# A two-layer transformer on one core: one tile for the output's sums of all passes, weights' sums at other slots, additions a slot apart, and a branch's number read sooner

## The chip, the cores and the metric

The kernel runs on one core of one Trainium2 chip. The time is the device time of one execution in microseconds (us), lower is better. The kernel before took 2757.16, 2756.16 and 2751.43 us in three runs; the median is 2756.16. Everything is in 32-bit floats.

The engines are written as in the profile: PE is TensorE (matmuls), ACT is ScalarE, DVE is VectorE, POOL is GpSimd, SP is the engine whose queue issues most of the transfers. A tile that a matmul writes (names ps_a, ps_b, ps_e, ps_sc, ps_o) lies in PSUM, and another engine must have read it before PE may fill it again.

## The reference

Two layers over 2048 tokens of 512 features. Each layer is attention plus a feed-forward part on the normalised input. The change touches only the first layer's attention (32 heads of 128):

```
qkv   = silu(xn @ qkv_w.T)                  # per head: q, k, v
per block of 32 tokens, with a state kv:
  out = (q k^T * diag_decay) v + (q * q_decay) kv
  kv  = kv * block_decay + (k * k_decay)^T v
attn  = norm_w * out_all * rsqrt(mean(out_all^2) + eps)
x1    = x + (sigmoid(xn @ gate_w.T) * attn) @ out_w.T + experts(xn)
```

The feed-forward part of layer one picks 2 of 16 experts for each token. Layer two is a 4-head softmax attention over sequences of 512, and 16 of 64 low-rank adapters for each token.

## The kernel before, in words

**Tiling.** Layer one's attention goes in four passes of 512 tokens (two sequences of 256), called pass 1 to pass 4 here; in the code the index `i` runs from 0, so pass 2 is `i == 1`. A pass has eight units `g`, 0 to 7, of four heads. A unit multiplies the tokens with that unit's weights for q, k, v and gate. This matrix product is done in sevenths, as Strassen and Winograd do: seven products of sums of blocks (`p1` to `p7`) in place of eight, and the sums that make up the results. In a unit the seven outer products come in the order p1, p2, p6, p5, p3, p7, p4 (the class `Outer`). From pass 2 on each of them is itself done sevenfold (in pass 1 only some are). That makes 49 small products in a unit, each of eight 128x128x256 matmuls in PE's records (L738), about 0.89 us, and around them the small attention of the four heads. A unit of pass 2 takes about 74.5 us.

In the span, the first decay load of pass 2 is at 707.3 us and that of pass 3 at 1303.4; pass 4 begins near 1880, and layer two near 2470.

**What happens to a product.** ACT copies one PSUM tile out (`copied`, L1112, cp<-ps_a), DVE adds the next to it, and DVE and POOL add the sum r to the results c (L101 is the line of the helper `add`). For p7 each of the four results is added twice: POOL adds r to the tile c, and DVE adds r to the tile a. The DVE additions are kept in a list `added`; three are issued together at the third result, and the fourth at the last. When a whole quarter of the results is complete, ACT makes silu and the gate (L835 to L842), PE makes scores and attends (L860/861, L872/873), DVE multiplies the scores by the decay (s, L101) and makes the gated result gT (L893), ACT squares and POOL sums the squares (sums), and POOL makes sums of gT for the next product.

**The output.** gT times the output's weights (L950, `project`) is sevenfold as well. The seven products are summed over the eight units in one tile `acc` of seven slots: unit 0 writes a slot by a copy on ACT (L958), later units add on DVE. Each pass takes its own tile from the pool `accp`, which has one buffer. After a pass, in unit 0 of the next, POOL combines the sevenths (`combine`, acc<-acc), and DVE adds them to the residual (`finish`, L649, spare<-acc,rms,spare).

**The output's weights.** Four of the seven products need sums of two weight blocks (wo<-wo). In pass 2 they are made by POOL in `out_sum` and each is stored to HBM by a transfer on SP (L1011, wos<-wo); the later passes load them. `load_out` loads the plain blocks, at the fourth, fifth and sixth outer product of the unit (k = 3, 4, 5).

**The order.** After each of the 49 products `slot()` is called. `later(after, f)` queues a piece of work for a later slot, and `slot` takes what is due: one piece, or two when over 12 wait, not counting pieces in a list of cheap names. The program order of ACT and POOL is the order in which the kernel issues (they are scheduled by hand); PE, DVE and SP are ordered by a planner by its own costs. Each engine then runs its instructions strictly in that order.

**The branch.** The router's number of expert tiles is known only at run time. In pass 4 each engine loads it (L1215) and jumps over extra experts if the usual number is enough (`beyond`, L1216).

## Time and profile before

| | us |
|---|---|
| median of three runs | 2756.16 |
| the profiled execution | 2759.92 |
| its span | 2758.2 |
| PE busy | 2704.0 (98%) |
| DVE busy | 1597.3 (58%) |
| POOL busy | 1652.5 (60%) |
| ACT busy | 943.9 (34%) |
| 32 weights' sums on POOL (wo<-wo) | 43.8 |
| mean granted TensorE clock | 0.994 |

A line of a timeline gives the start, the duration, the engine, the program's line, the operation, the tile written and the tiles read, how many instructions are drawn together, and in brackets how long the engine had been idle before it and what released it. A line of the list of waits gives the engine, what it wanted to do, after the arrow what it waited for, then microseconds in total, how often, and the longest.

### The profile page before, as it was taken

To read this page: it belongs to the slowest core of one execution; us is meant where nothing else is said; L and a number is where in the kernel's file an instruction comes from. 1 tells how busy PE (TensorE), PEld (TensorE's weight loads), DVE (VectorE), ACT (ScalarE), POOL (GpSimd) and SP (SyncE) were. 2 spreads that over 40 slices of the span, in tenths; PEclk is the share of its full clock that TensorE was granted. 3 is DMA by queue.
4 is the path that set the end of the run, shared out by engine and by line. 5 is a ranking of instruction groups with operands and counts; after the bars stand their busy time and mean duration, and the time that the engine had idled before them with its cause. 6 is when DMAs were issued, how large, how long until landed. Compare 5 with 4: busy or idle time off the path is not lost. (4 is left out here: it accounts for less than half of the span.)

```text
span 2758.2 us, 48688 instructions
## 1 busy us (share of the span) xinstructions
PE 2704.0 (98%) x19250; PEld 2499.6 (91%) x19250; DVE 1597.3 (58%) x2701; ACT 943.9 (34%) x1672; POOL 1652.5 (60%) x1509
## 2 busy tenths in 40 slices
PE   9999999999999999999999999999999999999999
PEld 5699999999999999999999999999998999987877
DVE  7656777776545555555545555555454555667663
ACT  5232222222343333333433333334433333432211
POOL 6478777776466767666755555656655567653210
PEclk9999999999999999999999999999999999999999
DMA  7898888888888777667777776787776688653211
GB/s 290 314 345 323 317 330 330 326 319 323 340 286 293 265 277 275 256 243 285 279 255 260 252 260 251 265 297 254 267 266 231 241 301 300 220 222 104 75 60 64
DMA packets 150872, 721.46 MB, mean 262 GB/s; under 512 B 18240, under 2 KB 24768, under 8 KB 108096
## 3 DMA queue, kind: packets, MB, share of 16 engines
q1 hardware_dynamic: 135824, 661.89, 65.2%
q0 software_dynamic: 14528, 55.88, 6.1%
q8 instruction: 154, 2.52, 0.4%
q14 instruction: 78, 0.64, 0.1%
q10 hardware_dynamic: 288, 0.52, 0.1%
HBM read 576.29 MB, written 144.04 MB: 261 GB/s over the span
## 5 line engine op out<-in xcount | busy, mean ns | idle before, releaser
L738 PE MATMUL ps_a<-xt,w 128*128 128x128 f32 x5376 | 752.1, 277 | 16.6 <-ACT cp L1112 11.8
L738 PEld LDWEIGHTS ps_a<-xt,w 128*128 128x128 f32 x5376 | 687.3, 193 | 44.5 <-ACT cp L1112 16.0
L101 POOL TENSOR_TENSOR c<-c,r 128x512 f32<-128x512 f32 x264 | 362.4, 1396 | 161.2 <-DVE r L101 157.7
L101 POOL TENSOR_TENSOR c<-c 128x512 f32<-128x512 f32 x240 | 305.8, 1286 | 254.4 <-DVE c L101 230.5
L1112 ACT COPY cp<-ps_a 128x512 f32<-128x512 f32 x384 | 224.2, 584 | 645.9 <-PE ps_a L738 620.0
L738 PE MATMUL ps_e<-xt,w 128*128 128x128 f32 x2688 | 376.1, 277 | 0.2 <-DVE r L101 0.2
L101 POOL TENSOR_TENSOR sums<-sums,sq 128x256 f32<-128x256 f32 x240 | 180.3, 751 | 307.7 <-ACT sq L884 297.9
L738 PE MATMUL ps_a<-w,xt 128*128 128x128 f32 x1792 | 348.0, 276 | 0.0
L738 PEld LDWEIGHTS ps_e<-xt,w 128*128 128x128 f32 x2688 | 342.9, 193 | 3.6 <-DVE r L101 0.4
L101 POOL TENSOR_TENSOR w<-w 128x512 f32<-128x512 f32 x224 | 298.2, 1339 | 76.4 <-DVE w L101 29.1
L950 PE MATMUL ps_sc<-wo,gT 128*128 128x256 f32 x1288 | 306.9, 382 | 5.2 <-PEq L1216 3.8
L738 PEld LDWEIGHTS ps_a<-w,xt 128*128 128x128 f32 x1792 | 273.3, 193 | 0.0
L101 DVE TENSOR_TENSOR acc<-ps_sc,acc 128x512 f32<-128x512 f32 x208 | 142.7, 689 | 207.0 <-PE ps_sc L950 164.2
L950 PEld LDWEIGHTS ps_sc<-wo,gT 128*128 128x128 f32 x1288 | 233.9, 192 | 31.6 <-issue 4.4
L893 DVE SCALAR_TENSOR_TENSOR gT<-ps_o,nw,c 128x256 f32<-128x256 f32 x256 | 112.0, 479 | 231.0 <-ACT sq L884 230.9
L738 PE MATMUL ps_b<-xt,w 128*128 128x128 f32 x1536 | 215.6, 277 | 6.0 <-issue 3.8
L101 DVE TENSOR_TENSOR c<-ps_a,c 128x512 f32<-128x512 f32 x216 | 146.8, 687 | 123.3 <-PE ps_a L738 117.6
L835 ACT ACTIVATE c<-c 128x512 f32<-128x512 f32 x256 | 150.2, 628 | 165.5 <-DVE c L101 108.0
L884 ACT ACTIVATE sq<-ps_o 128x512 f32<-128x512 f32 x128 | 76.5, 597 | 380.2 <-PE ps_o L873 371.8
L738 PEld LDWEIGHTS ps_b<-xt,w 128*128 128x128 f32 x1536 | 196.5, 193 | 9.2 <-issue 5.6
L101 DVE TENSOR_TENSOR s<-ps_sc,decay 128x384 f32<-128x384 f32 x256 | 139.1, 552 | 75.7 <-PE ps_sc L861 74.1
L738 PE MATMUL ps_e<-w,xt 128*128 128x128 f32 x896 | 174.1, 276 | 0.0
(296 smaller groups left out, 4581.7 us busy)
## 6 DMA issues: line engine op xcount, KB each, us to landing
w<-in_w_att_dram SPq DMA_DIRECT2D x56, 1024.0 KB
w<-in_w_att_dram SPq DMA_DIRECT2D x72, 768.0 KB
st<-in_w_att_dram SPq DMA_DIRECT2D x32, 1024.0 KB
wo<-in_w_out_dram SPq DMA_DIRECT2D x113, 256.0 KB
decay<-dec SPq DMA_DIRECT2D x64, 384.0 KB
w<-ws0p SPq DMA_DIRECT2D x12, 1792.0 KB
w<-ws1p SPq DMA_DIRECT2D x12, 1792.0 KB
w<-ws2p SPq DMA_DIRECT2D x12, 1792.0 KB
```

Source lines behind the costliest of these rows:

```text
L101: (eng or nc.vector).tensor_tensor(o, a, b, op)
L738: mm(bank[:, bass.ts(ty, P)], a, b, start=(first and ty == 0), stop=True, skip_group_check=True,)
L835: nc.scalar.activation(qk, qk, AF.Silu)
L884: nc.scalar.activation(sq, po, AF.Square)
L893: nc.vector.scalar_tensor_tensor(gT[:, h, :].rearrange("p (t n) -> p t n", t=2), po[:, bass.ts(h, S)].rearrange("p (t n) -> p t n", t=2), ...
L950: mm(py[:, bass.ts(t, S)], self.O[p][:, hh, bass.ts(t, P)], self.wo[p][:, hh, :], start=(t == 0 and hh == 0), stop=(hh == 1), skip_group_c ...
L1112: nc.scalar.copy(c, bank)
```

## The change

1. `acc` is one tile for all passes, taken once (`sums_of_seven`).
2. The output weights' sums of the second pass: the last plain block is loaded at k = 4 in place of k = 5, and the four sums are queued 6, 22, 24 and 26 slots later (slots 34, 50, 52, 54 of the unit, the last three in the next unit) in place of slots 41, 43, 45, 47.
3. p7's additions to the tile a: of the three that were issued together at the third result, one is issued at once, and the others are queued for one and two slots later; they count as cheap pieces. The fourth stays at the last result.
4. The branch's number is loaded at the start of the unit before the one that branches.

```diff
+    whole_acc = []
+
+    def sums_of_seven():
+        if not whole_acc:
+            whole_acc.append(accp.tile([P, 7, 2, C // 2], FP, tag="acc", name="acc"))
+        return whole_acc[0]
...
-                n += getattr(f, "func", f).__name__ not in ("bias_sum", "silu", "bias", "gate", "fill_tile", "read_table", "take_table", "scatter", "load_sum", "sums1", "sums2", "sums3", "sums4", "settle0", "settle1", "out_sum", "combine", "finish", "store")
+                n += getattr(f, "func", f).__name__ not in ("add_a", "bias_sum", "silu", "bias", "gate", "fill_tile", "read_table", "take_table", "scatter", "load_sum", "sums1", "sums2", "sums3", "sums4", "settle0", "settle1", "out_sum", "combine", "finish", "store")
...
                 if self.i not in acc:
-                    acc[self.i] = accp.tile([P, 7, 2, C // 2], FP, tag="acc", name="acc")
+                    acc[self.i] = sums_of_seven()
...
-                for p in {2: ("p1",), 3: ("p7", "p4", "p5"), 4: ("p6", "p2"), 5: ("p3",)}.get(k, ()):
+                for p in {2: ("p1",), 3: ("p7", "p4", "p5"), 4: ("p6", "p2", "p3")}.get(k, ()):
...
-                if k == 5 and self.i == 1:
+                if k == 4 and self.i == 1:
                     for n in range(4):
-                        later(6 + 2 * n, partial(self.out_sum, n))
+                        later((6, 22, 24, 26)[n], partial(self.out_sum, n))
...
+        def add_a(a, r):
+            add(a, a, r)
...
-                        self.added.append(partial(add, a, a, r))
-                        if (i, j) in ((1, 1), (0, 1)):
-                            while self.added:
-                                self.added.pop(0)()
+                        self.added.append(partial(add_a, a, r))
+                        if (i, j) == (1, 1):
+                            for n in range(3):
+                                later(n, self.added.pop(0)) if n else self.added.pop(0)()
+                        elif (i, j) == (0, 1):
+                            self.added.pop(0)()
...
+        n_used = []
+
         def beyond():
-            n_used = nc.values_load(used[0:1, 0:1], min_val=0, max_val=NMT)
-            with tc.If(n_used > USUAL):
+            with tc.If(n_used[0] > USUAL):
...
+            if (i, g, k) == (NCH - 1, NG - 6, 1):
+                n_used.append(nc.values_load(used[0:1, 0:1], min_val=0, max_val=NMT))
             if (i, g, k) == (NCH - 1, NG - 5, 1):
                 assert not todo
                 beyond()
```

More of the change, by code (lines that the diff above doesn't have):

```diff
@@ L974, in project_plain @@
                 if self.i not in acc:
-                    acc[self.i] = accp.tile([P, 7, 2, C // 2], FP, tag="acc", name="acc")
+                    acc[self.i] = sums_of_seven()
                 o = acc[self.i][:, 2 * b : 2 * b + 2, t]
```

## The prediction

> **What bounds the kernel now.** I read the share of busy time first, then the slices, then the list of what TensorE waited for.

> ```profile
> span 2758.2 us, 48688 instructions
> PE 2704.0 (98%) x19250; PEld 2499.6 (91%) x19250; DVE 1597.3 (58%) x2701; ACT 943.9 (34%) x1672; POOL 1652.5 (60%) x1509
> PEclk9999999999999999999999999999999999999999
> ```

> TensorE (PE) is busy 98% of the span at full clock, and the change has as many matmuls as before. So it can only give back, or add, gaps between matmuls, and the wait list of PE prices them (total us, times, longest).

> ```profile
> PE ps_a L738 <- ACT cp L1112: 11.8, 6, 2.6
> PE ps_o L872 <- DVE s L101: 6.2, 6, 2.6
> PE ps_b L738 <- issue: 3.8, 2, 2.0
> PE ps_sc L950 <- PEq L1216: 3.8, 1, 3.8
> PE ps_sc L950 <- POOL gT L101: 1.4, 1, 1.4
> ```

> The first row is the largest: six times a product waits for a PSUM tile that ScalarE (ACT) has not yet copied out. PE's timeline puts these at 125.23 (1.83 us, in the opening, which no edit touches), 1156.19 (1.77), 1230.73 (1.77), 1305.27 (1.11), 1360.30 (2.65) and 1938.35 (2.65). The last five are 9.95 us, of two kinds.

> At 1360.30, and alike at 1938.35, one unit into passes 3 and 4:

> ```profile
> 1359.18 0.58 ACT L958 COPY acc<-ps_sc 128x512 f32<-128x512 f32 x1 [8.66 <-DVE spare L649]
> 1360.30 0.94 PE L738 MATMUL ps_a<-xt,w 128*128 128x128 f32 x6 [2.65 <-ACT cp L1112]
> 1355.66 3.41 DVE L649 SCALAR_TENSOR_TENSOR spare<-acc,rms,spare 128x512 f32<-128x512 f32 x2 [0.56 <-POOL acc L101]
> 1358.99 0.68 DVE L101 TENSOR_TENSOR c<-ps_a,c 128x512 f32<-128x512 f32 x1
> ```

> ACT stands at the first copy into the new pass's sums (L958) until VectorE (DVE) has finished with the old pass's (L649). Two copies of products queue behind it, and PE wants the tile that they free.

> At 1156.19, and alike at 1230.73 and 1305.27, the starts of units 6 and 7 and of pass 3:

> ```profile
> 1148.39 3.07 POOL L101 TENSOR_TENSOR wo<-wo 128x512 f32<-128x512 f32 x2
> 1151.42 1.27 POOL L101 TENSOR_TENSOR c<-c,r 128x512 f32<-128x512 f32 x1
> 1152.64 1.29 POOL L101 TENSOR_TENSOR wo<-wo 128x512 f32<-128x512 f32 x1
> 1152.72 1.15 ACT L835 ACTIVATE c<-c 128x512 f32<-128x512 f32 x2 [5.01 <-POOL c L101]
> 1156.19 0.94 PE L738 MATMUL ps_a<-xt,w 128*128 128x128 f32 x6 [1.77 <-ACT cp L1112]
> ```

> GpSimd (POOL) does the sums of output weights (wo<-wo) between p7's last additions. ACT's silu (L835) waits 5.01 us for the last addition, five ACT operations follow, and only then the copy for PE.

> **Part 1: one tile for the output's sums.** Before, a new tile may be written only when the old one is released as a whole, thus after the last finish. With one tile, the copy waits only for what touches its own seventh: PE's product (ended about 1353.4) and the POOL sum that reads the old values (1350.32 + 2.50 = 1352.8). So the copy starts near 1353.5 instead of 1359.18. The gap goes twice. A PE row of six after a gap takes 0.94, elsewhere 0.83: 0.11 more. 2 x (2.65 + 0.11) = **5.5 us**. Late next is DVE's c<-ps_a,c, which stays behind the finishes: it ends at 1358.99 + 0.68 = 1359.67 and frees another ps_a tile. PE, now 2.7 us earlier, wants that one near 1360.4. Slack about 0.7; if it is negative, part of the gap comes back there, at most all of it.

> **Part 2: the sums at slots 34, 50, 52, 54 instead of 41 to 47.** 32 sums, 43.8 us of POOL in all, 1.37 mean; none is removed. In each unit three sums (1.27 + 3.07 = 4.3 us at 1143.80 and 1148.39) leave the stretch ahead of the silu, which covers most of its 5.01 wait and more than the 1.77 that reached PE. Gain: 1.77 + 1.77 + 1.11 + 3 x 0.11 = **5.0 us**. In units 0 to 5 PE had no such gap, so they give nothing.

> The sums now stand elsewhere on POOL, each 1.27 alone. Slot 34: POOL idles there for 1 to 4 us. Slots 50 to 54 are the first of the next unit, beside the chain sums, gT, whose product (L950) PE waits for. There:

> ```profile
> 859.14 1.28 POOL L101 TENSOR_TENSOR gT<-gT 128x512 f32<-128x512 f32 x1
> 864.78 1.54 POOL L101 TENSOR_TENSOR sums<-sums,sq 128x256 f32<-128x256 f32 x2 [4.37 <-ACT sq L884]
> ```

> Two sums (2.54) fit into this 4.37; at unit 6 the same idle time is 2.34, 0.2 too few. Bounds over eight units: 0 when hidden, 1.27 each (10.2) if every one pushes gT that PE has no slack for; the whole row PE <- POOL gT is 1.4 us now, so nearly 0: I take 0. Each sum also issues a store on SP's queue, and SP waits there for POOL. Behind it now comes a 1792 KB weight load (issued at 1155.15; at the slices' 300 to 345 GB/s it alone takes 5 to 6 us, and with the loads ahead of it I put its landing near 1164; its first product is near 1171). In the changed program it follows the second store, not the fourth, so 1 to 4 us later; slack about 7. Cost 0. The sums are read from slot 57 on (p7), three slots of 1.5 us after the last one.

> [...]

> ```profile
> 760.96 0.69 DVE L101 TENSOR_TENSOR c<-c,r 128x512 f32<-128x512 f32 x1
> 762.76 3.47 DVE L101 TENSOR_TENSOR c<-c,r 128x512 f32<-128x512 f32 x2
> 766.85 0.67 PE L872 MATMUL ps_o<-s,c 128*128 128x256 f32 x2 [2.56 <-DVE s L101]
> ```

> 0.69 alone, 1.73 beside POOL. [...]

> **Part 3: p7's additions a slot apart.** On DVE the new order differs only by a gather's copy ahead of an addition in some units, and at the starts of passes 3 and 4 by additions between the r's, as pass 2 has it already. No PE gap there hangs on it: 0 (bounds: -4.4 if it dissolved the gap at 766.85, 2.56 + 0.11 and the slow clock after it, 5.1 us x (1 - 0.67) = 1.7; +1 if one s falls behind one more 0.69 to 1.73 addition).

> **Part 4: the branch's number read sooner.** Only ACT's and POOL's loads move up a unit; PE's and DVE's stay directly before the compare. PE's 3.8 us (PEq L1216) is the compare itself, so **0** (bound -0.5, the 490 ns of the load). ACT's load costs about 0.47 where ACT is idle 2.19 before its next copy.

> **The clock.** [...] The trace is less clear: after the 2.56 gap the granted clock is 0.67 for 5.1 us, after the 2.65 gap 1.00 (1360.3 to 1366). For the five gaps removed the clock was 1.00, so nothing is added. If every one carried the 1.7 of the gap at 766.85, the sum would be 8.5 more; no row shows it.

> **Sum.** 5.5 + 5.0 = 10.5 us off the profiled 2759.9 (span 2758.2, 1.7 around it), thus 2749.4. That execution is 3.8 above the median of the runs, 2756.2, so the median becomes **2745.7 us**. Its own range is 2741 to 2750. 0.2%, 5.5 us, is about what tells a change from none.

> **Rivals.**
> - Half of it (chance 0.20). One gap returns at the next wait: DVE's c<-ps_a,c behind the finishes (slack 0.7) takes part 1's 5.5, or POOL's longer start of a unit takes part 2's 5.0. For: both margins are under 1 us. Against: the c<-ps_a,c ran 0.69 beside POOL, not held. 2750.7 to 2751.2, on the bound, half faster and half same.
> - More (0.13). The gap at 766.85 goes as well: 2745.7 - 4.4 = 2741.3. For: POOL is lighter there. Against: the same two additions stay ahead of s.
> - No change (0.05). The moved sums push gT in all eight units, 10.2 against 10.5: 2755.9. Against: 4.37 idle.
> - Slower (0.10). SP's queue: the weight load of each unit of pass 2 issues behind the fourth store (slot 54, near 1164) instead of the second. It then lands near 1173, 2 us after it is wanted; eight units make 16: 2745.7 + 16 = 2761.7. It decides once the load issues more than 7 us late, after 1162. For: SP already stood 6.72 us at these stores. Against: the order of the queue has two stores ahead, not four.

> Likeliest 0.52. Faster: 0.52 + 0.10 + 0.13 = 0.75; same 0.10 + 0.05 = 0.15; slower 0.10. Range: from 2738 (More, with the load's 0.5 and a held addition's 1.0 and some scatter) to 2758, beyond no change, leaving most of the slower case out.

> **What the changed profile would show.** ACT's copy into acc no longer waits for spare; PE ps_a <- ACT cp falls from 11.8 to about 1.8, one time; silu's wait on POOL at the unit starts falls from 5.0 below 3; POOL gT stays under 2 us; the gap near 767 and the 3.8 at the branch stay. I am wrong if a new PE row of several us stands for DVE c, POOL gT or a DMA of w in pass 2.

## The result

The changed kernel takes 2740.96 us in the median of five runs (2737.60 to 2747.29), against 2756.16 before: a ratio of 0.9950, 95% interval 0.9938 to 0.9962, so 10.5 to 17.1 us less. The same kernel run again later gave 2742.31 and 0.9941 (0.9926 to 0.9956). It is faster by more than the 0.2% that can be told, the forecast of 2745.7 lies inside the measured spread, the median lies at the lower edge of the forecast's likeliest range of 2741 to 2750, and the gain is some 3 to 5 us larger than the 10.5 of the sum. Where those came from is the question below.

The list of PE's waits in the changed kernel (lines are numbered differently here: L738 is now L745, L950 is L957, L872 is L879, L1112 is L1122, L835 is L842, L958 is L965):

```profile
PE ps_o L879 <- DVE s L101: 5.2, 5, 1.9
PE ps_sc L957 <- PEq L1229: 3.2, 1, 3.2
PE ps_a L745 <- ACT cp L1122: 2.8, 3, 1.9
PE ps_sc L957 <- POOL gT L101: 1.3, 1, 1.3
```

The row PE <- ACT cp, 11.8 us in six waits before, is 2.8 in three: the 1.9 of the opening, and two of 0.45. The rows for the branch, for s and for gT are still there. On ACT's side, the list of waits of the kernel before has these rows for the silu and for the copy into acc:

```profile
ACT c L835 <- POOL c L101: 57.5, 37, 5.0
ACT acc L958 <- DVE spare L649: 17.3, 2, 8.7
```

In the changed kernel the rows for the same two are:

```profile
ACT c L842 <- POOL c L101: 31.7, 32, 2.1
ACT acc L965 <- PE ps_sc L957: 49.7, 21, 4.0
```

The copy's wait for DVE's finishes (L649), 17.3 us in two waits, is gone from the list, and the longest wait of silu for POOL is 2.1 instead of 5.0. Compared with the profile before, place by place (the start of the same matmul in both), the gains are:

| stretch | gain in us | what it is |
|---|---|---|
| units 6, 7 of pass 2, start of pass 3 | 2.04 + 2.04 + 1.38 | the gaps of 1.77, 1.77, 1.11 |
| first units of passes 3 and 4 | 2.40 + 3.62 | the two gaps of 2.65 |
| units 1 to 5 of pass 2, small | 1.25 | waits for gT, and the matmuls beside them |
| first unit of pass 2, near 767 | 1.64 | its gap and what follows |
| the branch | 2.28 | its gap and what follows |
| pass 4, near 2229 | 0.71 | a wait of 0.45 for DVE r |
| opening and pass 1 | 3.00 | nothing that the change touches |
| layer two | 1.5 | the same |

The sum is 21.9, the difference of the two spans (2758.2 and 2735.9) to within 0.5. It is more than the medians show, since one trace of each kernel holds chance as well; the runs below take it apart as far as they can. From here on, a stretch in which the granted clock falls to about half is called a spell.

### The profile page after: what moved, and what is told of

Its sections match the earlier page's. It is cut to its first block, busy times and chain, and to the rows that moved or that the text cites. A ratio compares the mean times of both kernels' runs of the same rounds, so it can differ in the third digit from the quotient of the medians.

```text
span 2735.9 us, 48695 instructions
## 1 busy us (share of the span) xinstructions
PE 2694.2 (98%) x19250; PEld 2492.2 (91%) x19250; DVE 1592.9 (58%) x2701; ACT 944.6 (35%) x1672; POOL 1648.6 (60%) x1509
## 5 line engine op out<-in xcount | busy, mean ns | idle before, releaser
L745 PE MATMUL ps_a<-xt,w 128*128 128x128 f32 x5376 | 749.4, 276 | 6.5 <-POOL w L101 2.8
L745 PEld LDWEIGHTS ps_a<-xt,w 128*128 128x128 f32 x5376 | 685.7, 192 | 31.4 <-issue 14.6
L101 POOL TENSOR_TENSOR c<-c,r 128x512 f32<-128x512 f32 x264 | 360.1, 1388 | 164.3 <-DVE r L101 157.1
L1122 ACT COPY cp<-ps_a 128x512 f32<-128x512 f32 x384 | 224.4, 585 | 672.5 <-PE ps_a L745 630.8
L101 POOL TENSOR_TENSOR c<-c 128x512 f32<-128x512 f32 x240 | 305.6, 1286 | 250.2 <-DVE c L101 215.3
L745 PE MATMUL ps_e<-xt,w 128*128 128x128 f32 x2688 | 374.0, 275 | 1.1 <-DVE c L101 0.8
L101 POOL TENSOR_TENSOR sums<-sums,sq 128x256 f32<-128x256 f32 x240 | 180.6, 753 | 295.4 <-ACT sq L891 285.7
L745 PE MATMUL ps_a<-w,xt 128*128 128x128 f32 x1792 | 346.5, 275 | 0.0
L745 PEld LDWEIGHTS ps_e<-xt,w 128*128 128x128 f32 x2688 | 340.9, 192 | 5.6 <-DVE c L101 1.3
L101 POOL TENSOR_TENSOR w<-w 128x512 f32<-128x512 f32 x224 | 298.1, 1339 | 72.9 <-DVE w L101 25.3
L957 PE MATMUL ps_sc<-wo,gT 128*128 128x256 f32 x1288 | 304.8, 380 | 4.5 <-PEq L1229 3.2
L745 PEld LDWEIGHTS ps_a<-w,xt 128*128 128x128 f32 x1792 | 272.3, 192 | 0.0
L101 DVE TENSOR_TENSOR acc<-ps_sc,acc 128x512 f32<-128x512 f32 x208 | 142.6, 689 | 212.5 <-PE ps_sc L957 164.0
L957 PEld LDWEIGHTS ps_sc<-wo,gT 128*128 128x128 f32 x1288 | 232.4, 190 | 29.8 <-issue 3.3
L745 PE MATMUL ps_b<-xt,w 128*128 128x128 f32 x1536 | 215.4, 276 | 5.9 <-issue 3.7
L101 DVE TENSOR_TENSOR c<-ps_a,c 128x512 f32<-128x512 f32 x216 | 146.6, 686 | 116.6 <-PE ps_a L745 110.6
L745 PEld LDWEIGHTS ps_b<-xt,w 128*128 128x128 f32 x1536 | 196.1, 193 | 8.8 <-issue 5.5
L842 ACT ACTIVATE c<-c 128x512 f32<-128x512 f32 x256 | 150.1, 628 | 138.1 <-DVE c L101 106.3
L101 DVE TENSOR_TENSOR s<-ps_sc,decay 128x384 f32<-128x384 f32 x256 | 139.4, 552 | 79.9 <-PE ps_sc L868 78.5
L745 PE MATMUL ps_e<-w,xt 128*128 128x128 f32 x896 | 173.2, 275 | 0.0
```

The source lines that it names most:

```text
L101: (eng or nc.vector).tensor_tensor(o, a, b, op)
L745: mm(bank[:, bass.ts(ty, P)], a, b, start=(first and ty == 0), stop=True, skip_group_check=True,)
L842: nc.scalar.activation(qk, qk, AF.Silu)
L957: mm(py[:, bass.ts(t, S)], self.O[p][:, hh, bass.ts(t, P)], self.wo[p][:, hh, :], start=(t == 0 and hh == 0), stop=(hh == 1), skip_group_c ...
L1122: nc.scalar.copy(c, bank)
```

## The experiments

**1. Part 1 alone: one tile for the sums.** Edit to the kernel before:

```diff
-                    acc[self.i] = accp.tile([P, 7, 2, C // 2], FP, tag="acc", name="acc")
+                    acc[self.i] = sums_of_seven()
```

> The kernel before with part 1 alone: one tile for the output's sums. My sum: the two gaps of 2.65 at the first unit of passes 3 and 4 shrink to under 0.5 each, 5.5 us less, ratio near 0.998; pass 2 keeps its three gaps on ACT cp (1.77, 1.77, 1.11) and its 2.56 gap near 767. Rival, half of it: a gap of 2 or more returns within three products on DVE c<-ps_a,c, and the time stays within 2 us of before. Rival, the slow clock: the spells of granted clock near 0.65 after the 2.56 gap and after the branch come and go from one execution to the next, so they may be there or not, though nothing here touches them.

Measured: 2747.52, ratio 0.9974 (0.9965 to 0.9983), so 7.2 us less (4.7 to 9.6). In its trace both gaps of 2.65 are gone. What the half-gain rival feared came, but small: one wait of 0.45 for an ACT copy some products later in each of the two units, 0.42 more than the same place cost before. The gaps themselves thus gave 2.81 - 0.42 = 2.39 each, 4.8 in all, and yet the median moved by 7.2. At the second place the gain in the trace is 3.63, not 2.39. The timeline and the granted clock before say why. The table of stretches has, after the bounds, the length, the busy time of PE, PEld, DVE, ACT and POOL, the granted clock, the DMA's share and its GB/s; both stretches are of the kernel before, directly after its two gaps of 2.65:

```profile
1360.30:1364.30 4.00, 4.00 (x35) 4.00 (x36) 1.83 (x4) 3.16 (x5) 1.00 (x1) 1.00 0.99 305
1938.30:1942.30 4.00, 3.95 (x20) 3.95 (x21) 0.36 (x1) 2.55 (x4) 0.00 (x0) 0.57 0.99 308
```

The first is the one that the prediction took its 1.00 from: 35 matmuls in 4 us at that clock. After the second, equally long gap the mean clock was 0.57 and only 20 matmuls ran. PE's timeline before had it in plain sight: 1.34 us for a row of six at 1938.35, where the one at 1360.30 took 0.94.

```profile
1938.35 1.34 PE L738 MATMUL ps_a<-xt,w 128*128 128x128 f32 x6 [2.65 <-ACT cp L1112]
```

What a spell costs at these two places can be read by laying the traces side by side at the same matmuls. The products under it lose some 1.6 us, but about 0.4 of that comes back a few products later: without a spell PE waits there and starts slowly (0.12 at 1366.92), with one it does not. The net price is 1.24 to 1.28 in every pair of traces of which one has the spell and the other not.

**2. Part 2 alone: the weights' sums at other slots.**

```diff
-4: ("p6", "p2"), 5: ("p3",)
+4: ("p6", "p2", "p3")
...
-                if k == 5 and self.i == 1:
+                if k == 4 and self.i == 1:
-                        later(6 + 2 * n, partial(self.out_sum, n))
+                        later((6, 22, 24, 26)[n], partial(self.out_sum, n))
```

> The kernel before with part 2 alone: the weights' sums of pass 2 at slots 34, 50, 52 and 54, with the earlier load. My sum: 5.0 us less, all in units 5 to 7 of pass 2 (1.77, 1.77, 1.11 gone), ratio near 0.998; the two 2.65 gaps stay. If the sums also take away the small waits for gT in units 1 to 5 (0.21 each), 0.6 to 1.4 more. Rival that the sums free DVE near 767: the gap for s falls from 2.56 to 1.5 or less. Rival that part 2 shortens that gap just enough to keep the clock full: the gap is near 2.3 and the clock after it 1.00, 1.4 to 1.7 more. Slower rival: a wait of PE for a DMA of w or for POOL gT of over 1 us in each unit.

Measured: 2747.39, ratio 0.9966 (0.9952 to 0.9980), 9.4 us less (5.5 to 13.2). In the trace the three gaps give 2.04, 2.04 and 1.38, 5.46 in place of 5.0. Units 1 to 5 give another 1.25; most of it are three places where L950 waited 0.04 for gT and then started slowly (0.21, 0.10 and 0.08 of excess in a row). The two gaps of 2.65 stay. The expectation's rival on the gap near 767 fails on both counts: two gaps of 0.43 and 1.91 take the place of one of 2.56, so 0.2 less, and the clock fell after the second all the same. So the traces hold 6.7 us for part 2. That lies inside the interval; what the median shows beyond it is not told from noise by these runs.

**3. Part 3 alone: additions a slot apart.**

```diff
-                        if (i, j) in ((1, 1), (0, 1)):
-                            while self.added:
-                                self.added.pop(0)()
+                        if (i, j) == (1, 1):
+                            for n in range(3):
+                                later(n, self.added.pop(0)) if n else self.added.pop(0)()
+                        elif (i, j) == (0, 1):
+                            self.added.pop(0)()
```

> The kernel before with part 3 alone: p7's additions queued a slot apart. On DVE only the copy xeT moves ahead of one addition in four units, so my sum says 0, within 1 us in the trace's stretches outside slow-clock spells. Rival: the additions let s through near 767, and the 2.56 gap there falls below 1.

Measured: 2754.76, ratio 0.9999 (0.9990 to 1.0009). The gap near 767 is 2.56, as before.

**4. Part 4 alone: the branch's number sooner.**

```diff
-            n_used = nc.values_load(used[0:1, 0:1], min_val=0, max_val=NMT)
...
+            if (i, g, k) == (NCH - 1, NG - 6, 1):
+                n_used.append(nc.values_load(used[0:1, 0:1], min_val=0, max_val=NMT))
```

> The kernel before with part 4 alone: the branch's number loaded a unit sooner. My sum says 0: PE loads it directly before the compare as it did. Rival: the load that the other engines make sooner lets PE through earlier, so the 3.76 gap at the branch falls to the 3.17 of the changed kernel, and the clock after it stays full: 0.6 + 1.7 = 2.3 us less.

Measured: 2755.74, ratio 1.0001 (0.9992 to 1.0010). The wait at the branch is the longest of all twelve traces made here:

```profile
PE ps_sc L950 <- PEq L1217: 4.0, 1, 4.0
```

Over all twelve traces this gap ran from 3.08 to 4.04, with the number loaded early or late: 3.76 before, 3.17 and 3.55 in two profiles of the changed kernel, and 3.08, the least, in the sixth experiment below, which has no part 4. So the 0.6 in the result's table is no effect of part 4, and the other 1.7 is the clock again, which happened to hold after the branch in that profile. Of the twelve it held there in one more, that of the seventh experiment.

**5. A ladder of gaps.** In pass 3, which has almost no gaps of its own, ACT repeats a copy before the one that PE waits for. The repeats are extra work and change no result.

```diff
             def copied(self, bank):
                 c = attn.tile([P, 512], FP, tag="cp", name="cp", bufs=5)
+                u = self.u
+                if bank is self.a and not hasattr(self, "c1") and self.p in ("p1", "p5") and (u.i, u.g > 0) == (2, True):
+                    for _ in range([4, 5, 6, 7, 8, 9, 10][(2 * u.g + (self.p == "p5")) % 7]):
+                        nc.scalar.copy(c, bank)
                 nc.scalar.copy(c, bank)
```

> The changed kernel with PE gaps of known places in pass 3, where it has nearly none: in units 1 to 7, at p1 and p5, ACT repeats the copy of a product (same source, same target) 4 to 10 times before the one that PE waits for, 0.48 us each. I expect fourteen gaps of some 0.5 to 4 us. Theory: a gap under 2 is followed by full clock and costs its own length; one above 2.5 is followed, more often than not, by a spell of granted clock near 0.65 that costs another 1.7 (the traces so far: 0 of 8 after gaps of 1.77, 8 of 12 after 2.56 to 2.66). [...] Rival, pure chance: spells as often after 1.5 as after 2.6.

The one execution took 2744.15. The gaps came out at 0.05 to 0.65 only, so it tells nothing of long ones. In the program the planner had moved scores (L867/868) ahead of the product that waits, which filled the delay. None of these small gaps was followed by a slow spell.

**6. The first sum stays.**

```diff
-                        later(6 + 2 * n, partial(self.out_sum, n))
+                        later((6, 15, 17, 19)[n], partial(self.out_sum, n))
```

> The kernel before with the last three sums at slots 50, 52 and 54, but the first at slot 41 and the block still loaded at k = 5. Theory (the wait of ACT's silu is what counts): 3.07 us of POOL's work leave the stretch ahead of silu, so its wait falls from 5.0 to about 2, and the three gaps on ACT cp in units 5 to 7 of pass 2 vanish as in the second experiment: 5 us less. Rival (the sum at slot 34 and the early load are needed): a gap of 0.5 to 1.3 stays at units 6, 7 and pass 3.

Measured: 2748.26, ratio 0.9971 (0.9957 to 0.9984), 8.0 us less (4.4 to 11.9). Silu's wait at the start of unit 6, 5.01 us before, is here:

```profile
1147.42 1.15 ACT L835 ACTIVATE c<-c 128x512 f32<-128x512 f32 x2 [2.42 <-POOL c L101]
```

In the kernel with all of part 2 it is 0.74 there. The gains in pass 2 are the same 2.04, 2.04, 1.38 and 1.25. So the three sums ahead of silu were the cause, and neither slot 34 nor the earlier load is needed for the time.

**7. All four sums at slot 50,** directly ahead of the chain from the squares' sums to gT:

```diff
-                        later((6, 22, 24, 26)[n], partial(self.out_sum, n))
+                        later((22, 22, 22, 22)[n], partial(self.out_sum, n))
```

> The changed kernel with all four sums at slot 50, directly ahead of the chain sums, gT on POOL. In the changed trace gT ends at 1154.94 and PE's product with it starts at 1155.70, a slack of 0.76. Three sums more ahead of it are 3.8 us, so PE should wait 3.0 for gT in each of seven or eight units, 21 to 24 us more, and with a slow-clock spell of 1.7 after most of them 30 to 36: 2765 to 2776. Rival (the planner puts other products there, or the chain has more room than the trace shows): under 5 us more.

Measured: 2769.36, ratio to before 1.0048 (1.0033 to 1.0064). That is 28 us more than the changed kernel, inside the 2765 to 2776 expected. The list of PE's waits has this row; below it stands PE's timeline at two of the eight new gaps:

```profile
PE ps_sc L957 <- POOL gT L101: 22.0, 9, 3.2
```

```profile
779.76 1.56 PE L957 MATMUL ps_sc<-wo,gT 128*128 128x256 f32 x6 [2.44 <-POOL gT L101]
...
856.49 2.83 PE L957 MATMUL ps_sc<-wo,gT 128*128 128x256 f32 x8 [2.43 <-POOL gT L101]
859.10 1.06 PE L879 MATMUL ps_o<-s,c 128*128 128x256 f32 x2
859.96 0.64 PE L880 MATMUL ps_o<-s,c 128*128 128x128 f32 x2
860.38 1.09 PE L745 MATMUL ps_e<-xt,w 128*128 128x128 f32 x6
861.31 0.39 PE L745 MATMUL ps_e<-w,xt 128*128 128x128 f32 x2
```

The eight gaps are 20.7 us (22.0 less the one of 1.3 that every kernel has in pass 4). After the first the clock held: six matmuls in 1.56. After the second, as long to 10 ns, it did not: the rows from 856.49 to 860.38 take 2.83, 1.06, 0.64 and 1.09, where the same rows at full clock take 1.89, 0.60, 0.39 and 0.83. Five of the eight gaps had such a spell, 5 x 1.7 = 8.5; together 29. This is the mechanism of the rival "No change", with its true price: the chain had 0.76 us of room and the three sums were 3.8.

**8. The gap near 767 attacked directly.** In the first unit of pass 2, DVE's three additions come after the s that PE waits for, by a fixed order:

```diff
+        def add_kept(a, r):
+            tc.keep_in_program_order(nc.vector.tensor_tensor(a, a, r, ALU.add))
...
-                                later(n, self.added.pop(0)) if n else self.added.pop(0)()
+                                later(3 + n, partial(add_kept, *self.added.pop(0).args)) if (u.i, u.g) == (1, 0) else later(n, self.added.pop(0)) if n else self.added.pop(0)()
```

> The changed kernel with one more edit: in the first unit of pass 2, DVE's three additions of p7 come after the multiplications s that PE waits for near 764, instead of before. Theory: the gap of 1.91 there and the 0.42 before it vanish, and with them the spell that sometimes follows: 2.3 to 4 us less, near 2738. Rival: the additions come late for POOL's next work on the tile a, or for the results r, and a gap of 1 to 3 comes back within ten products; time unchanged.

Measured: 2739.84, ratio to before 0.9942 (0.9927 to 0.9956), not to be told from the changed kernel's 0.9950 and 0.9941. PE's timeline from 754 to 777 has these gaps:

```profile
756.49 0.94 PE L745 MATMUL ps_a<-xt,w 128*128 128x128 f32 x6 [0.78 <-DVE r L101]
767.74 0.94 PE L745 MATMUL ps_a<-xt,w 128*128 128x128 f32 x6 [0.85 <-DVE r L101]
776.10 1.13 PE L957 MATMUL ps_sc<-wo,gT 128*128 128x256 f32 x4 [0.53 <-POOL gT L101]
```

With another of 0.09 at 759.05 they are 2.25, where the changed kernel had 0.42 + 1.91 = 2.33: the gap was cut in pieces and not removed. The rival holds. The one thing won may be that no piece is long enough for a spell: none came here, but one profile cannot tell.

**9. A longer ladder:** as the fifth, with 12 to 24 repeats in place of 4 to 10.

> The ladder again with 12 to 24 repeats of the copy in place of 4 to 10, since those gave gaps of only 0.1 to 0.65. I expect gaps of about 1 to 5 us in pass 3. Theory from the ten traces so far: no spell of slow clock below 1.8 (none so far), one after some 6 in 10 of the gaps between 1.9 and 2.7, after nearly every one above 3; each spell costs 1.7 on top of the gap. [...] Rival, something of the places themselves (a change of pass, the branch) makes the spells, not the length: none in pass 3 whatever the gap.

Gaps of up to 9.3 us came, at a total of 2823.18 in the one execution. In pass 3, no spell after 0.54, 0.68 and 1.88; one after each of 2.93, 3.12, 3.91, 4.16, 4.35 and the longer ones. The stretch after the gap of 4.35:

```profile
1369.40:1374.00 4.60, 4.60 (x21) 4.60 (x22) 2.24 (x4) 3.43 (x7) 2.00 (x2) 0.50 0.26 108
```

So the place does not make the spell: pass 3's ordinary units have them once the gap is there.

**10. The changed kernel again,** without an edit.

> The changed kernel as it stands, once more on the same chip as the ladder: ratio near 0.995 as before. For the trace: the same gaps of 0.45 at the first unit of passes 3 and 4, and about 2.3 in two gaps near 762, of which the second (1.91) may or may not be followed by a spell this time, and one after the branch, whose gap should lie between 3.1 and 4.0 as in every kernel, whoever loads the number sooner.

Ratio 0.9941, given above. The same two gaps near 762 as in the first profile of it (0.43 and 1.91), and this time the clock fell. First the stretch after the 1.91 in this profile, then in the other:

```profile
762.80:767.80 5.00, 4.97 (x25) 4.70 (x26) 0.35 (x1) 0.59 (x1) 0.00 (x0) 0.66 0.91 357
```

```profile
763.80:768.80 5.00, 4.95 (x40) 4.88 (x41) 0.84 (x2) 2.15 (x4) 0.43 (x1) 1.00 0.89 343
```

One program, one place, the same gap: 25 matmuls in 5 us or 40.

**All twelve traces together,** every PE gap of over 1 us between 700 and 2440 us (layer one from pass 2 on), by its length, and how many were followed within 6 us by a spell (over 1.2 us lost by the granted clock; a spell is 1.7 us in most cases, more after the longest gaps):

| gap, us | gaps | with a spell |
|---|---|---|
| 1.1 to 1.8 | 25 | 0 |
| 1.88 to 2.7 | 26 | 16 |
| 2.9 to 3.31 | 8 | 6 |
| over 3.33 | 16 | 16 |

```profile
1358.44:1361.86 3.42, 1.56 (x14) 1.56 (x14) 1.23 (x2) 1.87 (x4) 1.76 (x2) 1.00 0.62 230
1361.86:1365.27 3.41, 3.41 (x33) 3.41 (x32) 2.81 (x5) 3.38 (x6) 1.97 (x2) 1.00 0.96 288
1935.30:1938.71 3.41, 0.76 (x7) 0.57 (x6) 2.42 (x3) 1.48 (x3) 2.94 (x2) 1.00 0.27 111
1938.71:1942.12 3.41, 3.41 (x19) 3.41 (x18) 0.18 (x1) 1.96 (x4) 0.00 (x0) 0.50 0.96 283
```

The grid cuts the first gap in two, so PE is idle for 1.86 of one stretch, and the clock holds. The second gap falls into one stretch, 2.65 idle, and the clock is 0.50 in the next. The two profiles of the changed kernel differ in the same way near 763: in the first, which kept its clock, one stretch holds 1.80 of the gap of 1.91; in the other, which had the spell, one holds all of it. Over the 75 gaps of the table, none of the 36 with at most 1.89 of idle time in any one stretch was followed by a spell, and of the 39 with 1.91 or more 38 were; the one exception has 1.94. The limit is read from these same gaps, with PE's ends as the profile models them, and no further run tested it. The grid lies elsewhere in these two executions, and so one program at one place can go either way.

## Why the prediction was right, and by how much it was short

**What bounds the kernel, and both mechanisms, held.** The five gaps named as the whole prize vanished, each with the edit it was put down to: the two of 2.65 with part 1 alone, the three others with part 2 alone. What waits next at passes 3 and 4 was another ACT copy, 0.45, and not DVE's c<-ps_a,c; the slack of 0.7 was enough.

**Parts 3 and 4 at nothing** held, with ratios of 0.9999 and 1.0001.

**The step that failed is the clock.** It said: "For the five gaps removed the clock was 1.00, so nothing is added", and "no row shows it". I had read the clock after one of the five and a row did show it, the 1.34 at 1938.35. In the five traces that still have the gaps of 2.65, six of ten such gaps were followed by a spell, at a net price of 1.25 there. Removing one therefore gives, on average, 2.39 + 0.6 x 1.25 = 3.1, and part 1 is 6.3 in place of 5.5; measured alone, 7.2 (4.7 to 9.6). The gaps proper gave less than booked, 4.8 in place of 5.5, since a wait of 0.45 for an ACT copy came in each unit. That this loss makes up for half of the missed clock in the sum is luck. Here gaps of 1.88 to 2.7 brought a spell in 16 of 26 cases. No stretch of the grid of 3.41 had to be idle as a whole: some 1.9 us of it was enough, with a spell after 38 of the 39 gaps that had 1.91 or more in one stretch and after none of the 36 that had less. An estimate from 3.41 and 1.9 alone, for a grid that may lie anywhere, gives a gap of 2.65 a spell in 66 of 100 cases, against six of ten counted.

**A term left out.** The small waits for gT in units 1 to 5, put at "so nearly 0: I take 0" with the sums taken to threaten them, fell instead, by 1.25. The three longer gaps gave 5.46 in place of 5.0: at 1156.19 the row behind the gap of 1.77 moved up by 1.94, and the rows behind that by 0.10 more.

**The sum, mended:** part 1 6.3, part 2 5.46 + 1.25 = 6.7, in all 13.0. The ratio 0.9950 is 13.8 (10.5 to 17.1), that of the second measurement 16.3 (12.1 to 20.4). The sum lies in both intervals, and what is left over cannot be told from noise by these runs. The 1.64 near 767 and 1.7 of the branch's 2.28 in the first comparison of profiles were spells that the profile before had and this one of the changed kernel had not. The gap near 767, now 1.91 in place of 2.56, may have a spell less often (three of four traces with 1.91, four of five with 2.56); that is too few to book.

**The two DVE additions near 767** were as slow as before. POOL's own additions moved up into the place that the sum had left, and the two took 3.47 us again:

```profile
758.00 4.69 POOL L101 TENSOR_TENSOR c<-c,r 128x512 f32<-128x512 f32 x3 [3.02 <-DVE r L101]
759.76 3.47 DVE L101 TENSOR_TENSOR c<-c,r 128x512 f32<-128x512 f32 x2
```

Why they take 1.73 each, where the one before them takes 0.69, no run shows. The 0.69 was not alone: in the kernel before, that addition ran from 760.96 and one of POOL's beside it from 761.00, for 1.79. The range of the prediction goes down to 2738 also for "a held addition's 1.0"; no run shows that term, and what the runs showed in its place is 3.47 before and after. Where the moved sums lie now they run at their shortest: wo<-wo averages 1271 ns in place of 1369, and the longest takes 1287 in place of 1729.

**Rivals.** "Half of it" and "Slower" did not come: no row for a DMA of w stands among PE's waits in pass 2, though a load now follows the second store. "No change" is a real mechanism, but with 0.76 us of room; experiment 7 shows what it costs past that. What "More" hoped for, the gap near 767, did not go; the gain above the sum came another way, by the clock and the small waits.

## What to carry to other kernels

Price a TensorE gap at its own length plus the chance of what follows it: read the granted clock after every such gap, not after one, and in several executions if there are any. In these traces a gap under 1.8 us costs itself; one near 2.65 costs 0.8 to 1 us more on average (six spells in ten, of 1.25 to 1.7); all 16 above 3.33 had a spell. By the grid, only from twice 1.9, some 3.8 us, must a gap fill enough of one stretch; that is an estimate. So cutting one long wait into short ones can pay even when their sum stays, if the pieces do not fall into the same stretch; no run here measured that gain by itself.

When work is moved along an in-order engine, look for whom it stood in front of and whom it will stand in front of, and measure the room there: the same four sums made the kernel 0.3% faster at one set of slots, and 1.0% slower than that (2769.4 against 2741.0, all else equal) at another, where 3.8 us of POOL's time stood ahead of a chain with 0.76 to spare.

When a comparison of two profiles shows more gain than the medians, look for places that the change doesn't touch, and for spells that one execution has and the other not, before crediting an edit.

## What was not expected of the hardware

Gaps equal to some 30 ns, at the same instruction, are followed by full clock in one execution and by half of it for 3.41 us in the next (2.65 to 2.68 us: six of ten), which goes with where the grid of 3.41 us falls: 74 of the 75 gaps fit a limit of some 1.9 us of idle time within one of its stretches. And the branch's gap on PE varied between 3.08 and 4.04 us over twelve traces, with no edit that accounts for it; what sets it stays open.
